# A macaron layer with mixture-of-experts halves: blank stores per attention group, and a dense expert sum on VectorE

## The chip, the cores and the metric

The kernel runs on one core of one Trainium2 chip. The metric is device time in microseconds (us), as the median of several executions. One further execution is taken by the hardware profiler; its page and its trace are the views that this document reads. In them PE is TensorE's products, PEld its weight loads (they lie beside the products), DVE is VectorE, ACT is ScalarE, POOL is GpSimd and SP is SyncE, which here only issues transfers. An engine name with a q (SPq) is that engine's own queue of instructions, from which transfers are started.

## The reference, cut to what matters

The input x holds 8 sequences of 256 tokens of 128 numbers. A feed-forward half with experts, attention, and the same feed-forward half again are added to it:

```python
def ffn(xt):                                   # xt: 2048 tokens x 128
    scores = softmax(xt @ router_w)            # 8 experts
    weights, idx = top_k(scores, 2)            # the two best
    h = gelu(einsum('td,edf->tef', xt, w1)) * einsum('td,edf->tef', xt, v1)   # F = 352
    y = einsum('tef,efd->ted', h, w2)
    return sum(weights[:, :, None] * take_along_axis(y, idx[:, :, None], 1), 1) + bias

x = x + 0.5 * ffn(layernorm(x))
x = x + attention(layernorm(x))                # 16 heads of 8, rotary, alibi, softmax
x = x + 0.5 * ffn(layernorm(x))
```

So each token needs only two of the eight experts, and the kernel may choose between computing those two alone and computing all eight and weighting six of them with zero.

## The kernel before, in words

**Stages.** Two feed-forward parts (part 0 and part 1) stand around attention. The tokens are kept in four blocks of 512 (two sequences each, `xb` and `x2`); a tile is 128 tokens. The expert weights are all in SBUF (`wall`), with F padded to three columns of 128.

**A part by rows.** For a block, `ffn_prep` computes the layer norm (`ln_stats`, with a power on GpSimd; `ln_apply`; `ln_turn`, which transposes on TensorE) and then `route` (L694) picks two experts per token, works out a row number for each choice, and GpSimd scatters the normalised token (`xs<-rows`, an indirect transfer, L731) into the region of its expert in a DRAM buffer `xs`. `wave` (L816) turns the counts into a table of tiles. `Tiles` (L908 to L1034) then runs one tile of 128 rows after another, each of one expert: SP loads it (`xr<-xs`), TensorE transposes it (`xT`), VectorE copies that expert's weights (`ws`, L958), TensorE makes g and v, ScalarE applies the Gelu (`gs`), VectorE multiplies, TensorE makes y (L988), ScalarE scales by the row's weight (`yo`), and GpSimd scatters the row to its token's place in a second DRAM buffer `ys` (L999). Since the number of rows of an expert is known only on the chip, the region's places without a token must hold harmless rows: they point at spare places of `ys`. `no_rows_anywhere` (L647) fills a whole region of part 1's `xs` with such blank rows, 1105 KB in one store from the tile `blank`, one store for each of the 8 experts, issued from SP's queue. The scatters of part 1 (L731) must follow these stores.

**The first sequence.** Part 0 doesn't wait for routing to begin with: sequence 0 (two tiles, unit (0, 0, 2) of `UNITS`) goes through all eight experts in `all_experts` (L745 to L783) while the other sequences are normalised and routed. This makes 16 products, k = 2e + t for expert e and tile t. Each has six products for g and v (`dg`, `dv`), a Gelu on ScalarE and a multiplication on VectorE (`dgs`), and three products into `dy`, in the one bank of tag O of the PSUM pool `ps_c`. `share` holds each token's weight for each expert, zero where the expert was not chosen. Before the change, ScalarE copies `dy` times `share` into `dyo` in SBUF (pool tag yg, two buffers, one for each expert), and when both tiles of an expert are there TensorE adds them to the running sum `dsum` (the bank of tag C) by a product with the identity. One VectorE addition puts `dsum` on the tokens at the end.

**Attention** runs as 32 groups, n = 0 to 31, four heads of one sequence each (`group`, L1202): s on TensorE, a bias and a minimum on VectorE (`ex<-s,alibi`), an exponential on ScalarE, transposes `eT`, copies `et`, then o on TensorE, evacuated by ScalarE (`og`), transposed and normalised by VectorE (`os`). After the fourth group of a sequence, `after` (L1283) makes the output projection `pr` and starts part 1's routing. Before a block can enter attention, its rows of part 0 are gathered: `ffn_sum` (L1036) loads `yg<-ys` on SP's queue and VectorE adds the two expert rows of each token to `xb` (`xb<-xb,yg`); `post1` (L1055) then makes the layer norm and `att_prep` (L1078) makes q, k and v. In the main loop (L1321 to L1345) `post1` of block b is planned with group 8b - 8 (block 1 with group 0), and the second half of block 0 with group 0.

**What sets the order.** Nothing runs as it is written. Each call only notes an operation with an engine, an estimated duration (`us`), an estimated landing time for transfers (`lands`) and a due time; `Plan` (L180 to L313) then schedules them: it takes, on every engine, the operation that can start earliest by its model, and among those that can start about as early, the one with the least due time (`plan.due`, set by `at(...)` or directly, in group numbers for attention). `plan.needs = [scored[n]]` says that what follows is planned after the s products of group n; it binds the planner's model alone and leaves no wait in the program. The engines then run their lists in that order, and the real waits are the data's. `Hand` (L317 to L347) records the operations, so most instructions of the trace have line L334. A buffer or PSUM bank that is taken again gives a wait as well.

The eight blank stores are noted in the main loop when n = 2:

```python
if n == 2:
    for e in range(E):
        no_rows_anywhere(part1, e)
```

Of the kernel before, what the change touches and what calls it, by code (L numbers as in the profile page):

```python
# [8 lines left out]
F32 = mybir.dt.float32  # L9
I32 = mybir.dt.int32  # L10
U32 = mybir.dt.uint32
AF = mybir.ActivationFunctionType
ALU = mybir.AluOpType
AX = mybir.AxisListType

P = 128
D = 128
E = 8
# [47 lines left out]
def tile_macaron(  # L66
# [22 lines left out]
    work = ctx.enter_context(tc.tile_pool(name="work", bufs=2))  # L89
# [3 lines left out]
    ps_c = ctx.enter_context(tc.tile_pool(name="ps_c", bufs=1, space=PS))  # L93
# [86 lines left out]
    class Plan:  # L180
# [33 lines left out]
        def group(self, us):  # L214

            plan = self

            class Group:
                def __enter__(self):
                    plan.one = Op(None, us, plan.due, 0.0)  # L220
                    plan.one.needs.update(plan.needs)
                    plan.ops.append(plan.one)
                    plan.due += plan.pace
                    return plan.one

                def __exit__(self, *_):
                    plan.one = None

            return Group()
# [85 lines left out]
    plan = Plan()  # L315
# [33 lines left out]
    te = Hand(nc.tensor, PE, 0.21)  # L349
    ve = Hand(nc.vector, DVE, 0.22)  # L350
    sc = Hand(nc.scalar, ACT, 0.3)
    gp = Hand(nc.gpsimd, POOL, 0.7)
    sy = Hand(nc.sync, SP, 0.5)
# [10 lines left out]
    def new(pool, shape, dtype, tag, name, bufs=None):  # L364
        def make():
            return pool.tile(shape, dtype, tag=tag, name=name, bufs=bufs)

        if plan is None:
            return make()
        return Late(Root(  # L370
            make, (pool.name, tag), bufs or pool.bufs, pool in (ps_a, ps_b, ps_c)
        ))
# [6 lines left out]
    def together(us):  # L379
        return plan.group(us) if plan is not None else nullcontext()  # L380
# [25 lines left out]
    def at(due, pace=0.0):  # L406

        plan.due, plan.pace = due, pace

    def fixed(shape, name):  # L410
        return new(const, shape, F32, name, name)
# [16 lines left out]
    for e in range(E):  # L428
# [5 lines left out]
        for c, cut in enumerate(CUTS):  # L434
# [4 lines left out]
                us=0.7, lands=8.0 if e < 4 else 12.0,  # L439
# [13 lines left out]
    ident = fixed([P, P], "ident")  # L453
# [30 lines left out]
    for b in range(NBLK):  # L484
        t = fixed([P, 2, TT, RW], f"rows{b}")
# [161 lines left out]
    def no_rows_anywhere(part, e):  # L647

        region = part.xs[REG * e : REG * (e + 1), :].rearrange("(n p) d -> p n d", p=P)
        own = blank[:, SPARE + e, :].unsqueeze(1).to_broadcast([P, REG // P, RW])  # L650
        part.blanked.append(sy.dma_start(region, own, us=0.5, lands=12.0 + 5.0 * e))

    def choose(part, n, xnT, tag):

        pl = scratch(f"rl_{tag}")[:, : n * E].rearrange("p (t e) -> p t e", e=E)
        for t in range(n):
            te.matmul(
                pl[:, t, :], xnT[:, t * P : (t + 1) * P], rw, start=True, stop=True, us=0.47
            )

        full, pair = [P, n, E], [P, 2, n, E]

        def some(name, shape, dtype=F32, bufs=None):
            return new(work, shape, dtype, f"r_{name}", f"r_{name}_{tag}", bufs)

        best, whose = some("best", full), some("whose", full, U32)
        with together(0.1 * n):
            for t in range(n):
                ve.max(best[:, t, :], pl[:, t, :])
        with together(0.14 * n):  # L670
            for t in range(n):
                ve.max_index(whose[:, t, :], best[:, t, :], pl[:, t, :])
        ex = some("sc", full)
        pick = some("pick", pair)
        for k in range(2):
            ve.tensor_tensor(
                pick[:, k], whose[:, :, k : k + 1].to_broadcast(full),
                experts.unsqueeze(1).to_broadcast(full), ALU.is_equal, us=0.15,
            )
        ve.tensor_tensor(ex, best, best[:, :, 0:1].to_broadcast(full), ALU.subtract)  # L680
        part.exps.append(sc.activation(ex, ex, AF.Exp, us=0.25))
        return pick, ex, some

    def halves(n, ex, some, out):

        sm = some("sm", [P, n])
        ve.tensor_reduce(sm, ex, AX.X, ALU.add)
        ve.reciprocal(sm, sm)
        ve.scalar_tensor_tensor(
            out.rearrange("p k t -> p t k"), ex[:, :, 0:2], 0.5,  # L690
            sm.unsqueeze(2).to_broadcast([P, n, 2]), ALU.mult, ALU.mult,
        )
# [52 lines left out]
    def all_experts(part, n, xt, xnT, tag):  # L745

        pick, ex, some = choose(part, n, xnT, tag)
        full, pair = [P, n, E], [P, 2, n, E]
        two = some("two", [P, 2, n])
        halves(n, ex, some, two)  # L750
        prod = some("prod", pair)
        ve.tensor_tensor(prod, pick, two.unsqueeze(3).to_broadcast(pair), ALU.mult)
        share = some("share", full, bufs=1)
        ve.tensor_tensor(share, prod[:, 0], prod[:, 1], ALU.add)
        total = new(ps_c, [P, n, D], F32, "C", "dsum")
        for e in range(E):
            yo = new(work, [P, n, D], F32, "yg", f"dyo{e}", 2)
            for t in range(n):
                k = n * e + t
                at(DUE_DENSE + NEXT_DENSE * k)  # L760
                pg = new(ps_a, [P, 3, P], F32, "A", f"dg{k}")
                pv = new(ps_a, [P, 3, P], F32, "A", f"dv{k}")
                for i, p in enumerate((pg, pv)):
                    with together(0.64):
                        for c in range(3):
                            te.matmul(
                                p[:, c, :],
                                wall[:, e, i * F + CUTS[c] : i * F + CUTS[c] + P],
                                xnT[:, t * P : (t + 1) * P], start=True, stop=True,
                            )  # L770
                gs = new(work, [P, 3, P], F32, "et" if k % 2 else "wide", f"dgs{k}", 8)
                sc.activation(gs, pg, AF.Gelu, us=0.49)
                ve.tensor_tensor(gs, gs, pv, ALU.mult, us=0.56)
                py = new(ps_c, [P, D], F32, "O", f"dy{k}")
                with together(0.66):
                    for c in range(3):
                        te.matmul(
                            py, gs[:, c, :], wall[:, e, 2 * F + c * D : 2 * F + (c + 1) * D],
                            start=(c == 0), stop=(c == 2),
                        )  # L780
                sc.activation(yo[:, t, :], py, AF.Copy, scale=share[:, t, e : e + 1], us=0.37)
            te.matmul(total, ident, yo, start=(e == 0), stop=(e == E - 1), us=0.41)
        ve.tensor_tensor(xt, xt, total, ALU.add, us=0.42)  # L783

    def ffn_prep(part, b, t0, n, xt, eng):

# [345 lines left out]
    for u, (b, t0, t1) in enumerate(UNITS):  # L1132
        at(DUE_UNITS[u], 0.1)
        ffn_prep(part0, b, t0, t1 - t0, xs0[b][:, t0:t1, :], sc)
        n = 2 * b + t1 // 2
# [35 lines left out]
    part1 = Part(1, NB)  # L1171
# [4 lines left out]
    plan = None  # L1176
# [3 lines left out]
    plan = Plan()  # L1180
# [140 lines left out]
    for n, (s, j) in enumerate(steps):  # L1321
        if j == 0:
            o = new(work, [P, 2, D], F32, "o", f"os_{s}", 3)
        last = group(n, s, j, o, ())

        plan.needs = [scored[n]]
        if n == 0:
            plan.due, plan.pace = 0.5, 0.018
            post1(0, ve, slice(1, 2))
            att_prep(1, ve)  # L1330
        if n == 2:
            for e in range(E):
                no_rows_anywhere(part1, e)
        for b in range(1, NBLK):
            if n == max(0, 8 * b - 8):
                plan.due, plan.pace = 8.0 * b - 8, 0.122
                post1(b, gp)
        if j == 0 and 1 < s + 1 < NB:
            plan.due, plan.pace = n + 0.2, 0.043
            att_prep(s + 1, gp)  # L1340
        plan.needs = []
        if j == 3:
            plan.due, plan.pace = n + 2.2, 0.046 if s + 1 == NB else 0.12
            after(s, o)
        plan.pace = 0.0  # L1345
# [9 lines left out]
    plan = None  # L1355
# [63 lines left out]
```

## Time and profile before

| what | value |
|---|---|
| median of 3 runs | 426.54 us (425.74 to 426.95) |
| the profiled execution | 423.09 us |
| its span, first to last instruction | 421.1 us |
| mean granted TensorE clock | 0.971 |
| PE busy | 376.8 us, 89% of the span |
| DVE busy | 314.0 us, 75% |
| ACT busy | 293.2 us, 70% |
| POOL busy | 241.4 us, 57% |
| dense sequence and part 0's tiles, 10 to 132 us | PE busy 117.37, DVE 84.19, ACT 73.04, POOL 66.99 |
| attention, 132 to 325 us | PE busy 179.35, DVE 169.88, ACT 173.72, POOL 122.12 |
| part 1's tiles, 325 to 405 us | PE busy 77.71, DVE 46.93, ACT 42.39, POOL 44.35 |
| end, 405 to 421 us | PE busy 0.56, DVE 5.54 |

The rows by stage are sums over a stretch of the span. How lines of the profile are read: on the page, a row of digits has one digit for each fortieth of the span (10.5 us), the busy share in tenths; PEclk is the TensorE clock that was granted, in tenths of full speed, and DMA the busy share of the 16 transfer engines. A row of the timeline gives the start in us, the length in us, the engine, the line, the operation with out<-in and the shapes, and in brackets how long the engine had been idle and what released it; "x8" gathers eight instructions in succession, whose length then runs from the first to the last. The chain that ended last is spread over many engines here (PE 11% of the span is its largest entry), so no single engine carries the whole kernel, and each stage is read by itself.

### The profile page before, as it was taken

The page shows a single profiled execution, that of the slowest core. Times are in us where ns is not written, and L with a number is a line of the kernel's source. Part 1 is how long each engine was busy: PE and PEld are TensorE (multiplying, and loading weights), DVE is VectorE, ACT ScalarE, POOL GpSimd, SP SyncE. Part 2 cuts the span into 40 slices and gives each one's busy share as a digit, 9 for nine tenths or more (in the row PEclk, how much of TensorE's full clock was granted, in tenths as well). Part 3 has the DMA queues.
Part 4 walks back from the last instruction along what each step waited for, and adds up shares of the span by engine and source line. Part 5 has one row for each costly group of instructions (what it writes and reads, how often), then busy time and mean ns, then how long its engine had stood idle before and what let it go on. Part 6 is the DMA issues. An engine that isn't in the chain of part 4 may idle for free. (4 is left out here: it accounts for less than half of the span.)

```text
span 421.1 us, 11473 instructions
## 1 busy us (share of the span) xinstructions
PE 376.8 (89%) x3456; PEld 317.2 (75%) x3456; DVE 314.0 (75%) x1348; ACT 293.2 (70%) x720; POOL 241.4 (57%) x323
## 2 busy tenths in 40 slices
PE   2989989999997789979999989999998999999940
PEld 1989979999996556755677666766667998999940
DVE  7766658888554898947998989899998677555515
ACT  3887555555555889965999989999999474555520
POOL 5267474547643086345857897687437757435430
PEclk9999989999999999996999999999999999999985
DMA  7971142211211999980000000011101222322117
GB/s 239 279 160 57 51 106 75 71 56 46 79 39 36 241 212 210 212 165 0 2 2 25 30 0 2 2 53 28 28 2 45 71 58 67 85 62 61 37 48 284
DMA packets 45053, 35.05 MB, mean 83 GB/s; under 512 B 4672, under 2 KB 41024, under 8 KB 44992
## 3 DMA queue, kind: packets, MB, share of 16 engines
q1 hardware_dynamic: 38608, 23.61, 25.7%
q0 software_dynamic: 4096, 8.46, 6.1%
q10 hardware_dynamic: 2288, 2.24, 1.5%
q8 instruction: 30, 0.49, 0.5%
q14 instruction: 31, 0.25, 0.2%
HBM read 14.27 MB, written 20.02 MB: 81 GB/s over the span
## 5 line engine op out<-in xcount | busy, mean ns | idle before, releaser
L334 ACT ACTIVATE ex<-ex,least 128x256 f32<-128x256 f32 x256 | 113.4, 508 | 4.8 <-DVE least L334 4.8
L999 POOL DMA_INDIRECT ys<-yo,xr x68 | 67.4, 991 | 63.0 <-ACT yo L334 50.3
L334 DVE CUSTOM_DVE_ANT_0 ex<-s,alibi 128x256 f32<-128x256 f32 x256 | 92.1, 418 | 8.1 <-PE s L334 7.2
L334 PE MATMUL eT<-ident,ex 128*128 128x128 f32 x512 | 74.2, 281 | 5.4 <-ACT ex L334 3.2
L731 POOL DMA_INDIRECT xs<-rows,r_at_f x60 | 58.7, 978 | 35.1 <-issue 14.4
L334 PEld LDWEIGHTS eT<-ident,ex 128*128 128x128 f32 x512 | 57.1, 142 | 24.6 <-ACT ex L334 8.9
L334 DVE TENSOR_TENSOR gs<-gs,v 128x384 f32<-128x384 f32 x68 | 37.3, 549 | 33.7 <-PE xT L334 25.0
L988 PE MATMUL y<-wall,gs 128*128 x408 | 57.2, 276 | 1.8 <-ACT yo L334 1.0
L334 PE MATMUL g<-xTs,ws 128*128 128x128 f32 x408 | 57.6, 278 | 1.0 <-DVE ws L958 1.0
L334 PE MATMUL v<-xTs,ws 128*128 128x128 f32 x408 | 57.3, 277 | 0.0
L334 PEld LDWEIGHTS g<-xTs,ws 128*128 128x128 f32 x408 | 51.7, 194 | 2.1 <-DVE ws L958 0.9
L988 PEld LDWEIGHTS y<-wall,gs 128*128 128x128 f32 x408 | 50.9, 192 | 3.0 <-ACT yo L334 1.4
L958 DVE COPY ws<-wall 128x704 f32 x68 | 37.4, 550 | 19.5 <-DVE gs L334 8.4
L334 PEld LDWEIGHTS v<-xTs,ws 128*128 128x128 f32 x408 | 51.7, 194 | 0.0
L334 ACT ACTIVATE gs<-g 128x384 f32<-128x384 f32 x68 | 33.3, 490 | 21.1 <-PE g L334 21.0
L334 ACT ACTIVATE yo<-y,xr 128x128 f32<-128x128 f32 x68 | 25.0, 368 | 31.3 <-PE y L988 28.4
L359 ACT COPY et<-eT 128x512 f32<-128x512 f32 x79 | 43.7, 583 | 3.7 <-PE eT L334 3.6
L334 PE MATMUL s<-kT,qT 32*128 32x256 f32 x512 | 40.7, 406 | 3.8 <-DVE least L334 3.1
L334 PEld LDWEIGHTS s<-kT,qT 32*128 32x128 f32 x512 | 25.4, 186 | 13.2 <-issue 6.1
L334 PE MATMUL o<-et,vp 128*32 128x256 f32 x512 | 35.1, 393 | 0.0
L334 POOL TENSOR_SCALAR qT<-qa,mask 128x256 f32<-128x256 f32 x32 | 29.8, 944 | 7.4 <-ACT qa L334 7.3
L359 DVE COPY et<-eT 128x512 f32<-128x512 f32 x49 | 32.3, 681 | 1.1 <-PE eT L334 1.0
(167 smaller groups left out, 596.3 us busy)
## 6 DMA issues: line engine op xcount, KB each, us to landing
xs<-blank SPq DMA_DIRECT2D x8, 1105.0 KB, 17.4
xr<-xs SPq DMA_DIRECT2D x68, 65.0 KB, 1.8
yg<-ys SPq DMA_DIRECT2D x3, 512.0 KB
wall<-in_w_dram SPq DMA_DIRECT2D x8, 176.0 KB, 5.1
wall<-in_v_dram SPq DMA_DIRECT2D x8, 176.0 KB, 3.0
yg<-ys SPq DMA_DIRECT2D x5, 256.0 KB
ys<-yo,xr POOLq DMA_INDIRECT x68
yg<-ys ACTq DMA_DIRECT2D x4, 256.0 KB, 4.6
```

The source lines that it names most:

```text
L334: lambda: f(*[real(x) for x in a], **{n: real(x) for n, x in k.items()}),
L359: (nc.scalar.copy if op.eng is ACT else nc.vector.tensor_copy)(real(out), real(in_))
L731: nc.gpsimd.indirect_dma_start(out=part.xs, in_=real(row), in_offset=None, out_offset=bass.IndirectOffsetOnAxis(ap=real(to)[:, k, t : t + ...
L958: nc.vector.tensor_copy(real(ws), flat(w, 2 * F))
L988: nc.tensor.matmul(real(py), real(hT)[:, c, :], flat(w + 2 * F + c * D, D), start=(c == 0), stop=(c == 2),)
L999: nc.gpsimd.indirect_dma_start(out=self.part.ys, in_=real(yo), in_offset=None, out_offset=bass.IndirectOffsetOnAxis(ap=real(xr)[:, D : D + ...
```

## The change

The change has two independent parts.

First, the blank stores of part 1. They were noted all eight at n = 2, in the planner's eyes after the s products of group 2, with landing times from 12 to 47 us. Now one is noted with each of the groups n = 2 to 9, due at n, each with a landing time of 9. Number, size, source and queue of the stores are the same.

Second, the sum over the experts of the first sequence. Before, ScalarE scaled each of 16 `dy` into `dyo`, TensorE added 8 times over the identity into `dsum`, and VectorE added `dsum` to the tokens. Now VectorE multiplies each `dy`, read from its PSUM bank, by the tokens' share and adds the tokens to it in one instruction (`scalar_tensor_tensor`, 16 of them, 128x128 each). `dyo`, `dsum`, the scalings, the identity products and the last addition are gone. The sixteen additions go to the same token tile in turn, expert after expert.

```diff
@@ -648,7 +648,7 @@
 
         region = part.xs[REG * e : REG * (e + 1), :].rearrange("(n p) d -> p n d", p=P)
         own = blank[:, SPARE + e, :].unsqueeze(1).to_broadcast([P, REG // P, RW])
-        part.blanked.append(sy.dma_start(region, own, us=0.5, lands=12.0 + 5.0 * e))
+        part.blanked.append(sy.dma_start(region, own, us=0.5, lands=9.0))
 
     def choose(part, n, xnT, tag):
 
@@ -752,9 +752,7 @@
         ve.tensor_tensor(prod, pick, two.unsqueeze(3).to_broadcast(pair), ALU.mult)
         share = some("share", full, bufs=1)
         ve.tensor_tensor(share, prod[:, 0], prod[:, 1], ALU.add)
-        total = new(ps_c, [P, n, D], F32, "C", "dsum")
         for e in range(E):
-            yo = new(work, [P, n, D], F32, "yg", f"dyo{e}", 2)
             for t in range(n):
                 k = n * e + t
                 at(DUE_DENSE + NEXT_DENSE * k)
@@ -778,9 +776,10 @@
                             py, gs[:, c, :], wall[:, e, 2 * F + c * D : 2 * F + (c + 1) * D],
                             start=(c == 0), stop=(c == 2),
                         )
-                sc.activation(yo[:, t, :], py, AF.Copy, scale=share[:, t, e : e + 1], us=0.37)
-            te.matmul(total, ident, yo, start=(e == 0), stop=(e == E - 1), us=0.41)
-        ve.tensor_tensor(xt, xt, total, ALU.add, us=0.42)
+                ve.scalar_tensor_tensor(
+                    xt[:, t, :], py, share[:, t, e : e + 1], xt[:, t, :], ALU.mult, ALU.add,
+                    us=0.3,
+                )
 
     def ffn_prep(part, b, t0, n, xt, eng):
 
@@ -1328,9 +1327,9 @@
             plan.due, plan.pace = 0.5, 0.018
             post1(0, ve, slice(1, 2))
             att_prep(1, ve)
-        if n == 2:
-            for e in range(E):
-                no_rows_anywhere(part1, e)
+        if 2 <= n < 2 + E:
+            plan.due = n
+            no_rows_anywhere(part1, n - 2)
         for b in range(1, NBLK):
             if n == max(0, 8 * b - 8):
                 plan.due, plan.pace = 8.0 * b - 8, 0.122
```

## The prediction on record

> **What bounds the kernel now.** I read the page's slices first, then busy time in windows, then the waits and the timeline at the two places where TensorE's clock falls. The slices show the dense product of the first sequence and part 0's tiles (10 to 132 us) with PE at 9 nearly throughout, attention (133 to 325) with PE and DVE both near 9, and one hole in slice 18, just where DMA falls from 9 to 0:
>
> ```profile
> PE   2989989999997789979999989999998999999940
> ...
> DVE  7766658888554898947998989899998677555515
> ...
> PEclk9999989999999999996999999999999999999985
> DMA  7971142211211999980000000011101222322117
> ```
>
> The windows (PE, PEld, DVE, ACT, POOL busy us, then clock, DMA share, GB/s) show both falls of the clock. DVE is busy for 1.99 and 2.33 of 5 us while the transfers drain:
>
> ```profile
> 55.00:60.00 5.00, 3.07 (x21) 2.78 (x20) 2.86 (x13) 3.33 (x8) 3.78 (x5) 0.89 0.60 133
> 60.00:65.00 5.00, 5.00 (x35) 4.90 (x35) 2.39 (x5) 1.85 (x6) 2.92 (x4) 0.77 0.33 88
> ...
> 180.00:185.00 5.00, 5.00 (x56) 3.42 (x52) 1.99 (x8) 4.53 (x14) 3.05 (x6) 1.00 1.17 213
> 185.00:190.00 5.00, 2.65 (x20) 1.77 (x16) 2.33 (x9) 2.12 (x6) 1.31 (x3) 1.00 0.28 103
> 190.00:195.00 5.00, 4.22 (x18) 2.60 (x19) 4.97 (x27) 2.18 (x6) 1.42 (x3) 0.70 0.00 0
> 195.00:200.00 5.00, 5.00 (x37) 3.40 (x36) 2.43 (x15) 3.10 (x8) 4.56 (x9) 0.62 0.00 0
> ```
>
> The timeline names the wait: block 2's expert rows (yg), queued on SP behind all eight blank stores.
>
> ```profile
> 136.73 37.02 SPq L334 DMA_DIRECT2D xs<-blank  x8
> 173.89 6.09 SPq L334 DMA_DIRECT2D yg<-ys  x2
> ```
>
> ```profile
> 187.67 0.69 DVE L334 TENSOR_TENSOR xb<-xb,yg 128x512 f32<-128x512 f32 x1 [5.32 <-DMA yg<-ys]
> ```
>
> **Change 1: the blank stores.** The group number is only the planner's: in the built order these stores wait for no engine, only for older transfers on their semaphores. So they aren't paced; SP still issues them back to back. What moves is one transfer: the order becomes yg of block 1, yg of block 0's second half, seven stores, yg of block 2, the eighth store, yg of block 3. VectorE's list in attention is the same row for row. No store is added.
>
> Price of a store: the eight and the loads among them occupy the queue from 136.7 to 187.7, 51 us. The 1.3 MB of yg take about 3.7 us of it at the 350 GB/s of 138 to 140 us; 47.3/8 = 5.9 us a store. Block 2's rows then land 5.9 us sooner relative to the attention, at 181.8 on the old scale. VectorE has its previous work done at 182.35, so the 5.32 us wait should vanish with 0.6 us to spare. Behind it goes what the wait caused: TensorE sat idle for 2.12 us before 189.11, its clock fell, and VectorE waited another 2.57 us for the slow projection (pr) at 199.38. Together 7.9. The check: the evacuations of o (og) of groups 7 to 9 start at 185.46, 198.54 and 203.59, 18.13 us for two groups; the other groups take 5.44 on average (181.49 us from first to last without the gaps of 13.08 and 10.63, over 29), so 18.13 - 10.88 = 7.2 is lost. I take **7.2** (bounds 5.3, the wait alone, and 9: groups 7 to 11 by the two best averages). What is late next: VectorE itself, and GpSimd with block 2's layer norm, which starts as much sooner. The eighth store and block 3's rows land some 3 us later at worst; the first reader of either, a scatter, runs at 222, and block 3's rows are added at 233.
>
> **Change 2: the dense sum.** Removed from TensorE: eight sums over the identity, 16 matmul passes. Their durations (380 ns) overlap, so I take the distance to the next start: 0.54, 0.54, 0.44, 0.43, 0.44, 0.44, 0.54, 0.43, **3.8 us** in all. Removed from ScalarE: 16 scalings at 0.36 = 5.8 us. Added to VectorE: 16 scale-and-adds of 128x128 out of PSUM; this form isn't in the trace. The 128x8 scale-and-add takes 0.16, the 128x256 addition of dsum out of PSUM 0.42, so 0.29 by the line between them (ends 0.16 and 0.42): 4.6 us, less the one 0.42. VectorE is busy 28 of 40 us there (15 to 55), so it can hold them, but in order: each waits for its product, and the next product for it, since their bank has one buffer.
>
> Does TensorE use the 3.8? Two sums (1.08) lie before 36 us, where ScalarE's table loads (1.28 each, at 25.15, 27.94, 32.56, 34.10) set the pace. In the built order the third block's power follows two scatters on GpSimd instead of one (1.26 later), so its normalised rows and the table loads behind them come later, while ScalarE's lost scalings there (0.6) pull the other way. TensorE's product after the third block's transposes, at 35.94 now, I put 0.75 later (between 0.75 later and 1.08 sooner). From there six sums remain, 0.44 + 0.43 + 0.44 + 0.44 + 0.54 + 0.43 = 2.72, and TensorE is the bound: +2.0 so far.
>
> Then the handover to the tiles. Now the sum at 57.99 waits 1.93 us for a scaling behind two table loads:
>
> ```profile
> 57.99 0.70 PE L334 MATMUL dsum<-dyo,ident 128*128 128x256 f32 x2 [1.93 <-ACT dyo L334]
> 58.53 1.15 PE L334 MATMUL dy<-wall,dgs 128*128 128x128 f32 x6
> ```
>
> The clock falls and the products up to 62.25 run slowly: dy 0.95 instead of 0.67 between starts, g and v 1.28 each, the transpose 0.21 instead of 0.13; 1.6 us lost. The loads stay, but the last dense product waits for a Gelu, not a scaling, and one more product and its hidden half stand before it: I estimate a wait of 1.1 (0 to 2.1), so 0.8 back, and the clock's 1.6, since a 1.63 us gap at 141.04 left it at 1.00. Sum: 2.0 + 0.8 + 1.6 = **4.4** (bounds -1 and 6.5). From tile 3 on TensorE runs at 2.12 us a tile until 132, so the gain is carried to attention; tile loads (each 1.8 us, some 1.5 apart from 50.0) stay ahead of it.
>
> **Sum.** 7.2 + 4.4 = 11.6. The profiled execution took 423.09 (span 421.1, 2 us around it), so 411.5 for its like; the median is 426.54, 3.5 higher, and I give it there: **414.9**.
>
> **The clock rule.** The row: the clock fell after gaps of 1.93 and 2.12 us. [...]
>
> **Rivals.**
> - *The rows are still late.* The DMA share falls slowly, 0.93 at 184.5 to 0.06 at 188: the transfer engines end at different times, and the slowest decides. For it speaks that slope and the thin 0.6 us; against it that the slowest also skips a store. If the wait stays by half with its clock fall, 3 to 4 us are lost: 418.5; wholly: 422.1. [...]
> - *The dense stage gains nothing.* ScalarE's loads and VectorE's order absorb the 2.72, or the clock falls at the handover all the same (1.6): 426.5 - 7.2 = 419.3, or 416.5.
> - *Slower: VectorE starves TensorE.* Each expert choice is a burst of about 2.3 us on VectorE (23.20 to 25.5). A product whose bank waits behind a burst leaves TensorE idle; from gaps of about 1.9 us on, the clock falls too, 1.6 more. There are four bursts; if all of them did both, 4 x 3.9 = 15.6 lost against 11.0 gained (7.2 and 3.8): 431.1. Against it: 2 to 4 us of other products stand between most such neighbours in the built order.
> - *Nothing to see:* the yg stays late and the dense gain is lost: 426.
>
> **Chances** (0.3%, 1.3 us, is about what can be told from no change). Forecast 0.56 (own range 411.5 to 418), dense stage gives nothing 0.13, rows still late 0.14, nothing 0.06, slower 0.11. Faster 0.83, same 0.06, slower 0.11. The range: below, all bounds at their best give 426.5 - 15.5 = 411; above, the late rows at 422.
>
> **What would show it.** Right: no DVE wait for yg at group 8 above 1 us; og 7 to og 9 in 11 to 12 us; no clock below 0.9 from 185 to 200; the first s product near 129; scale-and-adds of 0.29. Wrong: VectorE still waiting for yg, a clock fall before 60, TensorE waits above 2 us at third-block transposes, or s later than 132.

## The result and the profile after

| | median | runs |
|---|---|---|
| before | 426.75 us | 425.74 to 428.26, 4 runs |
| changed | 420.71 us | 419.29 to 421.36, 4 runs |

The ratio is 0.9851, 95% interval 0.9811 to 0.9891: the change saves 6.0 us. The forecast was 11.6 saved (414.9). The time lies in the stated range of 411 to 422, but only in the part that the rival of the late rows had added to it: the forecast's own range ended at 418. The gain is half of what was forecast. The profiled execution took 421.11, span 419.3.

Four lines of the page's slices (a digit for 10.5 us):

```profile
PE   2989989999997799989999989999999999999930
...
DVE  7778777889454798958899989899998776555515
...
PEclk9989999999998799996999999999999999999995
DMA  8971143311311999991001000011001222322117
```

The hole in PE's eighteenth digit (178 to 189 us) has gone from 7 to 8 and not closed, and PEclk still has the 6 right behind it. The sixth digit of PEclk, the handover, went from 8 to 9; but there are new falls in the third (an 8, near 28 us) and in the thirteenth and fourteenth (8 and 7, 134 to 144 us). The windows (busy us of PE, PEld, DVE, ACT, POOL, then clock, DMA share, GB/s) give the two stretches that the prediction looked at, and one of the new falls (140 to 145):

```profile
55.00:60.00 5.00, 3.56 (x32) 3.32 (x31) 3.23 (x14) 2.64 (x7) 3.78 (x5) 1.00 0.48 124
60.00:65.00 5.00, 4.93 (x44) 4.69 (x43) 3.79 (x13) 2.60 (x7) 3.78 (x5) 1.00 0.49 114
140.00:145.00 5.00, 4.93 (x42) 2.73 (x42) 4.66 (x28) 4.37 (x11) 0.62 (x1) 0.66 1.24 182
180.00:185.00 5.00, 5.00 (x54) 3.37 (x53) 1.38 (x4) 4.74 (x14) 3.31 (x7) 1.00 1.11 260
185.00:190.00 5.00, 3.46 (x18) 1.90 (x16) 4.63 (x22) 2.26 (x5) 0.18 (x1) 0.83 1.04 193
190.00:195.00 5.00, 5.00 (x29) 3.44 (x32) 4.47 (x26) 2.73 (x7) 3.72 (x5) 0.50 0.04 14
```

The clock fall at the handover (55 to 65 us) is gone: 1.00 against 0.89 and 0.77. From 185 to 195 there is a fall again, 0.83 and 0.50 where the profile before had 1.00 and 0.70, and DVE is busy for 1.38 of the 5 us from 180, less than the 1.99 before. The timelines of SP's queue and of VectorE say why:

```profile
134.59 35.60 SPq L334 DMA_DIRECT2D xs<-blank  x7
170.32 6.18 SPq L334 DMA_DIRECT2D yg<-ys  x1
176.54 0.72 SPq L334 DMA_DIRECT2D xs<-blank  x1
```

```profile
185.37 0.69 DVE L334 TENSOR_TENSOR xb<-xb,yg 128x512 f32<-128x512 f32 x1 [3.96 <-DMA yg<-ys]
```

The order in the queue is the one forecast, seven stores, the rows, one store; and VectorE still waits 3.96 us for the rows. Counted from the issue of the first store, they landed after 50.8 us here (185.37 - 134.59) and after 50.9 in the profile before (187.67 - 136.73): one store fewer ahead, and no sooner.

| step | before | after |
|---|---|---|
| tile 0's transpose xT | 55.79 | 56.50 |
| tile 3's transpose | 64.83 | 61.88 |
| first s product | 133.22 | 130.77 |
| og of group 0 | 143.46 | 142.61 |
| og 7 to og 9 | 18.13 | 16.16 |
| og of group 31 | 324.95 | 322.22 |
| last product y | 404.62 | 402.03 |
| end of span | 421.1 | 419.3 |

By these two profiles the change gains only 1.8 us, while the medians differ by 6.0. So the profiled execution of before was itself 3.5 us better than the median of its kernel, and what is to be found out is where those 3.5 us lie. In the first two sets of runs below the kernel before took 470 to 471 us, with standstills of several engines (last section); only ratios within a set are compared.

### The profile page after: what moved, and what is told of

Read it like the earlier page. It is cut to its first block, busy times and chain, and to the rows that moved or that the text cites. A ratio compares the mean times of both kernels' runs of the same rounds, so it can differ in the third digit from the quotient of the medians.

```text
span 419.3 us, 11415 instructions
## 1 busy us (share of the span) xinstructions
PE 375.8 (90%) x3440; PEld 315.6 (75%) x3440; DVE 318.5 (76%) x1363; ACT 288.3 (69%) x704; POOL 241.5 (58%) x323
## 5 line engine op out<-in xcount | busy, mean ns | idle before, releaser
L334 PE MATMUL eT<-ident,ex 128*128 128x128 f32 x512 | 75.1, 284 | 5.4 <-ACT ex L334 3.1
L334 ACT ACTIVATE gs<-g 128x384 f32<-128x384 f32 x68 | 33.3, 490 | 20.4 <-PE g L334 19.6
L334 PE MATMUL s<-kT,qT 32*128 32x256 f32 x512 | 41.7, 418 | 2.4 <-DVE least L334 1.5
L334 PEld LDWEIGHTS s<-kT,qT 32*128 32x128 f32 x512 | 25.9, 193 | 12.2 <-issue 6.4
```

What stands on the lines that cost most here:

```text
L334: lambda: f(*[real(x) for x in a], **{n: real(x) for n, x in k.items()}),
```

## The experiments

Theory: (1) a blank store costs about 6 us in SP's queue, in a typical execution of before the rows came some 5 us later than in the one that was profiled, and the stores make nearly the whole gain; (2) the dense sum gains 2 to 3 us at the first s, and little at the end. Rivals: the dense sum makes most of the gain; or the rows are late because the stores take the transfer engines, not because of their place in the queue.

**First set (before 471.1 us).** The kernel before, unchanged:

> The kernel before once more, unchanged. Its profiled execution took 423.09, 3.5 us under the median of 426.5. Theory A (the drain of the blank stores varies from one execution to the next, and the execution that was profiled had a short one): this profile takes about 426.5, and the wait for block 2's rows (yg) is longer than the 5.32 us of the first profile, 7 to 9. Theory B (the difference is elsewhere, for instance in where the clock falls): the wait is again 5 to 6 us and the 3.5 us show in other stretches, such as clock falls at other times.

Measured: 0.9983 (0.9952 to 1.0013). VectorE's wait for the rows:

```profile
212.01 0.69 DVE L334 TENSOR_TENSOR xb<-xb,yg 128x512 f32<-128x512 f32 x1 [10.18 <-DMA yg<-ys]
```

The wait is almost twice that of the first profile; og 7 to og 9 took 23.6 us instead of 18.13. The rows landed 56.3 us after the first store's issue (212.01 - 155.68), not 50.9. This speaks for theory A; but the execution also had standstills, which the first profile had not and neither theory names, so a third profile was taken below.

The stores alone (the dense part as before the change):

```diff
-        part.blanked.append(sy.dma_start(region, own, us=0.5, lands=12.0 + 5.0 * e))
+        part.blanked.append(sy.dma_start(region, own, us=0.5, lands=9.0))
...
-        if n == 2:
-            for e in range(E):
-                no_rows_anywhere(part1, e)
+        if 2 <= n < 2 + E:
+            plan.due = n
+            no_rows_anywhere(part1, n - 2)
```

> The stores of the change alone; the dense sum stays on ScalarE and TensorE. Theory A (one store fewer ahead of the rows is worth its share of the queue, and a typical execution of before waits longer than the profiled one): 3.5 to 4.5 us faster than before, so about 422.5, with a wait for yg of 2 to 5 us left. Theory B (the stores are worth only the 2.0 us that group 7 to group 9 gained between the two profiles): 424.5. My prediction had 7.2: 419.3 and no wait.

Measured: 0.978 (0.9708 to 0.9852). The wait fell from 10.18 to 1.64 us, og 7 to og 9 from 23.6 to 12.0, the rows landed after 50.1 us. The stores alone give as much as the whole change gave (0.9851 above, 0.9841 in the next set). A wait is left, as theory A has it, though under its 2 to 5 us; the gain, 7.4 us between the medians, is above both theories and near the 7.2 of the prediction.

The dense sum alone (the second part of the change, all eight stores at n = 2):

> The dense sum of the change alone; all eight stores stay ahead of block 2's rows. Theory A: the first s product comes 2.5 us sooner (130.8), and the time gains that or less, 424.0 to 425.0, because the eight stores start with the attention and the wait for yg moves with it. Theory B (the dense sum makes most of the measured 6.0 us): 421.5 to 422.5. My prediction had 4.4: 422.1.

Measured: 0.9993 (0.9958 to 1.0029), wait for the rows 10.31 us. The first s came at 154.24, later than before's 152.19. Theory B is out; that the standstills hid a gain can't be told from this run.

The rows ahead of all stores, with both parts of the change:

```diff
+        if n == 1:
+            plan.due = 1.0
+            for b in 2, 3:
+                ahead[b] = ffn_sum(part0, b)
+                next(ahead[b])
...
-            for _ in ffn_sum(part0, b, q):
+            for _ in ahead.pop(b, None) or ffn_sum(part0, b, q):
```

> Both parts of the change, and block 2's and block 3's rows loaded ahead of all eight stores (noted at group 1). If it is the place in SP's queue behind the stores that makes block 2's rows late, VectorE's wait for yg (3.96 us in the profile after) is gone, the distance from og 7 to og 9 falls from 11.3 and 4.9 us (16.2) to 11 or 12, no clock fall is left from 185 to 195, and the time is 4 to 5 us below after: 416. If the wait only uncovers another (GpSimd's layer norm of block 2, the shared transfer engines), the wait for yg goes and the sum of og 7 to og 9 stays above 14: 419 to 420.7. If the stores, now started some 10 us later, make part 1's scatters late, the time is 421 or more.

Measured: 0.9757 (0.9704 to 0.981). The two additions of the rows ran at 201.47 without a wait, og 7 to og 9 took 10.8 us, and no clock fall is left in that stretch (170 to 290 us all at 1.00). With no store ahead of them the rows are in time, and nothing else is late there. The stores started 10 us later (166.28 against 156.48 in the changed kernel's run of the next set) and nothing waited for them.

**Second set (before 470.2 us).** Before once more, and the changed kernel:

> The kernel before again, to see a third execution. In the first profile VectorE waited 5.32 us for block 2's rows, in the second 10.18, and there ScalarE also stood still four times for 3 to 7 us with nothing in the trace that released it. Theory A (the stores' drain varies): without such standstills the time is about 426 and the wait for yg lies between 5 and 10 us. Theory B (the drain is long only where ScalarE stands still): without standstills the wait is 5 to 6 us, with them about 10.

> The changed kernel again, on the same chip as the others of this call. Theory A: 6 to 9 us under before (the stores' 7.4 of the run with the stores alone, and the dense sum's 0 to 2.5); og 7 to og 9 at 12 to 16 us. If the dense sum adds to the stores in full, og 0 comes 2 us sooner than in before; if it gives nothing, og 0 comes as in before and the difference is that from og 7 to og 9 alone.

Measured: 0.9981 (0.9948 to 1.0013) and 0.9841 (0.979 to 0.9892). The wait in before was 10.19 us, the rows landed after 56.1 us; in the changed kernel 1.51 and 48.7. og 7 to og 9: 22.3 and 12.2. The first s came at 153.85 and 152.76, og 0 at 165.36 and 164.70. So here too the gain is the stretch of the rows. Both executions of before with the long wait had standstills, so these two alone don't exclude theory B (a long drain only with standstills); the drain of the stores in the executions without standstills, given below with the price of a store, does.

The dense sum alone, again:

> The dense sum alone, again. In the first run of it ScalarE stood still for 9.3, 5.0 and 6.2 us before 81 us, 20.4 in all against 17.6 in before, and the first s came at 154.2 against 152.2; the time was 0.9993 of before. Theory A (the product chain gains 2.5 us and the standstills hid it): without standstills the first s comes 2 to 3 us sooner than in before and the time is 1.5 to 2.5 us less. Theory B (VectorE's order takes back what TensorE saves): within 1 us of before, whether there are standstills or not.

Measured: 1.0017 (0.9972 to 1.0062), first s at 154.60, wait for the rows 8.16. There were standstills again (ScalarE 9.3, 5.0 and 4.0 us before 82 us), so its two theories weren't told apart.

Rows first, and two PSUM banks for dy:

```diff
-                py = new(ps_c, [P, D], F32, "O", f"dy{k}")
+                py = new(ps_c, [P, D], F32, "C" if k % 2 else "O", f"dy{k}")
```

> Rows of blocks 2 and 3 ahead of all stores, as before in this study, and the dense products dy in two PSUM banks by turns (the bank of the sum that is gone is free), so that a product needn't wait for VectorE's scale-and-add of the one before. If one bank is what holds the dense stage back, tile 0's transpose and the first s come another 1 to 1.5 us sooner than in the changed kernel (its wait of 1.44 us for VectorE at 58.21 goes) and the time is 3 to 5 us under the changed kernel; if the products wait for their own halves (dgs) all the same, the first s stays within 0.5 us and only the rows' gain of 3 us is left.

Measured: 0.976 (0.9691 to 0.983), first s at 150.34, the earliest of all with standstills. But ScalarE stood still for 8.8 us before 77 us here and for about 18 to 21 in the runs with one bank, so this first s says little about the bank.

**Third set (before 429.3 us, no standstill in any of its four profiles).**

The rows first (the edit above, and one store per group), with the dense sum of before:

> The rows of blocks 2 and 3 ahead of all eight stores, and the dense sum left on ScalarE and TensorE. Against the same order of loads with the dense sum on VectorE (0.9757 of before) it prices the dense part where no store is in the way. Theory A (the dense sum on VectorE is worth nothing with one PSUM bank for dy, since each product waits for VectorE's scale-and-add): 0.973 to 0.979 of before, the first s within 1.5 us of before's. Theory B (it is worth the 2.5 us at the first s of the profile after): 0.980 to 0.984.

Measured: 417.40 us, 0.9735 (0.9701 to 0.9769). The four stores ahead, with both parts (the load noted at n == 6 instead of 1):

> Both parts of the change with four stores ahead of the rows of blocks 2 and 3, and four behind. In the profiles so far block 2's rows landed 56.1 to 57.2 us after the first store was issued with eight stores ahead (50.9 in the very first profile), and 48.7 to 50.8 with seven. If a store costs 6 us in the queue, they land at 30 to 34 us, 15 us before VectorE asks for them, so the wait is gone and the time equals that with none ahead, 0.976. If the rows are late for another reason (the transfer engines shared with the stores), a wait of 1 us or more stays and the time is that of the changed kernel, 0.984.

Measured: 416.50 us, 0.9714 (0.9676 to 0.9752). SP's queue and VectorE in this kernel:

```profile
134.96 16.88 SPq L334 DMA_DIRECT2D xs<-blank  x4
151.95 7.20 SPq L334 DMA_DIRECT2D yg<-ys  x2
159.20 22.58 SPq L334 DMA_DIRECT2D xs<-blank  x4
```

```profile
178.98 1.87 DVE L334 TENSOR_TENSOR xb<-xb,yg 128x512 f32<-128x512 f32 x2
```

No bracket: VectorE didn't wait, though four more stores were still being written. The last packet of the rows of blocks 2 and 3 ended at 168.25, 33.3 us after the first store's issue, where 30 to 34 were expected. The windows of this kernel show no fall of the clock, with DMA shares above 1:

```profile
180.00:185.00 5.00, 4.74 (x51) 3.09 (x50) 4.93 (x23) 5.00 (x15) 4.02 (x7) 1.00 1.31 174
185.00:190.00 5.00, 4.58 (x54) 3.43 (x53) 4.96 (x27) 4.40 (x12) 3.85 (x8) 1.00 1.18 191
190.00:195.00 5.00, 5.00 (x58) 3.39 (x54) 4.87 (x26) 4.95 (x14) 4.94 (x7) 1.00 0.24 47
```

So stores that are being written behind the rows don't make them late; what makes them late is the number of stores ahead of them. That is as far as the rival of the shared transfer engines is tested: whether the same rows, loaded through another engine's queue beside the stores, would be in time was not tried. And the two kernels of this pair, neither with a late row, give a price for the dense sum, though they differ in the order of the transfers too: first s at 133.18 without it and 130.90 with it, 2.3 us sooner; og 0 at 143.57 and 142.16, 1.4; last y at 397.86 and 396.77, 1.1; the medians 0.9 apart, with intervals that overlap. Theory A for the first of them (worth nothing) had the ratio right; theory B (2.5 us of time) had the first s right and the time wrong. What the time has is about 1 us or nothing. The kernel with the rows first and two banks, below, has the same order of transfers as the first of them, and the new dense sum; between these two the first s comes 2.3 us sooner (133.18 and 130.92) and the medians lie 1.3 apart (417.40 and 416.09), again with intervals that overlap.

The two banks, with the stores as changed, and with the rows first:

> The changed kernel with the dense products dy in two PSUM banks by turns, and the stores as changed (seven ahead of block 2's rows). If the one bank holds the dense stage, the first s comes 2 to 3 us sooner than in the changed kernel and the time is about 0.977 of before (0.984 less 2 to 3 us); if the sooner first s of the run with two banks and the rows first (150.3 against 152.8 to 154.6) was chance, it is 0.982 to 0.986.

> Rows first and two banks, again. Its two numbers did not agree: a median of 457.1 (3 rounds), 13 us below before's, and a ratio of 0.976. If the two banks add to the rows' gain: 0.969 to 0.974 of before, first s at 150 to 151. If they add nothing: 0.976 to 0.980 and first s at 153 or later.

Measured: 423.55 us, 0.9864 (0.9827 to 0.99), first s at 130.09; and 416.09 us, 0.9686 (0.9659 to 0.9713), first s at 130.92. Against 130.77 (profile after) and 130.90 (four ahead) with one bank the second bank gives 0 to 0.8 us at the first s: one bank isn't what holds the dense stage. (The first s of 150 expected for the second kernel was meant for executions with standstills. Its ratio falls on the side of "they add", but its interval overlaps that of four ahead with one bank, 0.9676 to 0.9752.) The first of the two is also a second case of seven stores ahead without standstills:

```profile
186.05 0.69 DVE L334 TENSOR_TENSOR xb<-xb,yg 128x512 f32<-128x512 f32 x1 [6.17 <-DMA yg<-ys]
```

The rows landed after 52.0 us (186.05 - 134.09). It and four ahead differ in the place of the rows (and in the bank, worth little): 0.9864 against 0.9714, 6.4 us of 429.3. That is what the change leaves on the table.

The rows first with two banks, 416.09 us, beats both kernels: 13 us under before, where the change has 6. Neither part of the change was run alone without standstills; that the stores make nearly the whole gain rests on the two sets with them and on the stretch from og 7 to og 9.

## Why the prediction was half right

*The order of the transfers* was right: the stores aren't paced, and one transfer moved past one store.

*The price of a store*, 5.9 us, came out near, in part by luck. Landing of the rows (the start of the addition that waited for them) after the first store's issue, over all profiles in which VectorE waited for them:

| stores ahead | us after the first store's issue |
|---|---|
| 8 | 50.9 (the profile shown first), 56.3, 56.1, 57.2, 56.1 |
| 7 | 50.8 (the profile after), 50.1, 48.7, 52.0 |

The means are 50.4 with seven and, without the first profile, 56.4 with eight: 6.0 a store. But the last four with eight all had standstills, and of those with seven only the second and third, so the packets of the stores themselves are the better measure (17,408 of 520 bytes, 2,176 a store). From the end of the first store's packets to the end of the sixth's, a store took 5.4 us in the profile before, 6.2 in the profile after, and 6.0 to 6.6 in the eleven other profiles in which no rows lie between these six. The windows of the profiles before and after show it in GB/s, the last number:

```profile
145.00:170.00 25.00, 22.85 (x225) 15.39 (x224) 23.64 (x115) 22.75 (x60) 18.15 (x28) 1.00 1.23 211
145.00:170.00 25.00, 23.31 (x230) 15.94 (x229) 23.64 (x112) 23.08 (x60) 18.48 (x29) 1.00 1.25 184
```

At these rates 1105 KB take 5.4 and 6.1 us. The prediction's 5.9 was counted from the first issue to VectorE's addition, over a drain that was a fast one (the packets of its eight stores ran for 45.3 us, 5.7 a store): too long a stretch at too fast a rate, which offset each other. Without standstills a store took 6.2 to 6.6 us (four profiles), with them 6.0 to 6.3: the long drain doesn't need them. Why the drain of the first profile was fast is not known.

*The step that failed* is the one behind it: "Block 2's rows then land 5.9 us sooner relative to the attention, at 181.8 on the old scale", so that the wait "should vanish with 0.6 us to spare". The old scale was that of one execution, and in it the rows came 5.5 us sooner than in four others. That the profiled execution lay 3.5 us under the median was seen, and carried along as a constant. It was no constant: eight stores at 5.4 instead of 6.1 us each (the mean of the four others with eight ahead) make 5.6 us, about the 5.5, and they lie in the very wait that the change moves. With eight stores ahead og 7 to og 9 took 18.13 us in that profile and 20.3 to 23.6 in the other four, 22.2 on average, 4.1 more. All four had standstills. A second execution of before without them was not profiled; that its drain is long too is an inference, from the 6.2 to 6.6 us a store of the other kernels' profiles without standstills, and from the third set: there the rows in time gained 0.0265 of 429.3, 11.4 us, without the dense sum, where the first profile had only 18.13 - 10.75 = 7.4 to give. The difference of 4.0 is about the 3.5 between that execution and its median. From a typical execution the sum would have run: 56.4 - 5.9 = 50.5 after the first store, against VectorE being ready for the rows after 45.6 (182.35 - 136.73 in the first profile); so a wait of about 5 stays. That is the rival "the rows are still late", which had 0.14 and, by half and wholly, 418.5 and 422.1 us; the measured 420.71 lies between these. In all four profiles with seven stores ahead the wait stayed, 1.5 to 6.2 us; 3.96 in the profile after, with a fall of the clock behind it.

What lateness costs in all was near the estimate's shape: og 7 to og 9 without any wait takes 10.5 to 10.8 us in the five profiles with the rows in time (10.88 was expected). In the four executions with eight stores ahead and standstills 22.2 - 10.8 = 11.4 us are lost, as much as the rows alone gain in the third set. Change 1 takes about half of it (to 16.2 in the profile after; 12.0 to 19.3 in the three others with seven stores ahead), and that is about the whole 6.0.

*The dense sum*: 4.4 was forecast for attention's start, 2.45 came in the profile after (130.77 against 133.22), and 2.3 between the two kernels of the third set. Term by term: the product after the third block's transposes came at 36.89, 0.95 later (0.75 expected). The clock fall at 27.87, which the prediction didn't have, cost nothing there: with four ahead, which has the same dense stage and no fall, the product came at 36.99, after a wait of 0.99 for ScalarE. The six sums behind it went, but one product waited 1.03 us at 48.54 where 0.46 was lost before:

```profile
47.43 0.59 DVE L957 COPY ws<-wall 128x704 f32 x1 [0.48 <-issue]
47.95 0.54 DVE L334 TENSOR_TENSOR dgs<-dgs,dv 128x384 f32<-128x384 f32 x1
48.54 0.94 PE L334 MATMUL dy<-wall,dgs 128*128 128x128 f32 x6 [1.03 <-DVE dgs L334]
```

Its half (dgs) stood in VectorE's list behind the copy of a tile's weights (ws), before which VectorE itself was idle for 0.48 us; the expert choice came behind it, at 48.41. So it was the order in VectorE's list and not a full VectorE, though each scale-and-add took 0.35 us instead of 0.29. At the handover the wait is 1.44 (1.1 expected; the product's bank came free with a scale-and-add, behind a half that had waited 1.28 for its Gelu) and the clock stayed at 1.00, as expected (no fall there in the four profiles without standstills that have the new dense sum; one at 58.88 and 58.92 in the two that have the old one):

```profile
56.50 0.27 PE L334 MATMUL xT<-ident,xr 128*128 128x128 f32 x1
58.21 0.94 PE L334 MATMUL dy<-wall,dgs 128*128 128x128 f32 x6 [1.44 <-DVE x L334]
58.99 0.27 PE L334 MATMUL xT<-ident,xr 128*128 128x128 f32 x1
```

At tile 3 the gain was 2.95, at tile 4 2.6. "The gain is carried to attention" held to the first s and not behind it: in the profile after, the clock fell at 133.68 and again at 140.51, and og 0 was 0.85 sooner; in the third set, without these falls, og 0 was 1.4 sooner, because block 1's rows, loaded once part 0's last rows are written, were issued 1.9 sooner (134.01 against 135.94) and landed 1.4 sooner (138.10 against 139.51). At the end about 1 us is left. The rival "VectorE starves TensorE" showed in this one place, through a weight copy and not an expert choice, without a fall of the clock there, and was not what decided.

*The clock*: a fall at the handover was priced at 1.6 and went away; the three new falls of the profile after were not in the forecast. Up to 400 us the clock stood at 0.50 in these stretches: in the profile before from 58.88 for 3.41 us and from 192.00 for 6.83; in the profile after from 27.87, 133.68 and 140.51 for 3.41 us each, and from 188.29 for 6.83. The two starts of before lie 133.12 us apart, and the later three of after lie 105.81, 112.64 and 160.42 us behind its first; in lengths of the shortest fall, 3.41 us, these are 39.0, and 31.0, 33.0 and 47.0. The prediction's "from gaps of about 1.9 us on, the clock falls too" rested on two gaps and doesn't hold: the longest waits of TensorE in the 3.41 us ahead of the four falls of after were 0.54, 0.84, 1.60 and 0.94 us, while 1.44 us at 58.21, and 1.63 at 141.04 in the profile before, brought none. Nor does the busy time tell it: TensorE was busy for 1.5 to 2.6 us of the 3.41 ahead of each of the six falls, and with 1.82 us busy from 185.17 to 188.59 in the profile before no fall began at 188.59. What brings a fall was not shown.

## What to carry to other kernels

Where a profiled execution lies apart from the median of its kernel, find the stretch in which it differs before adding or subtracting in it; here the load behind eight stores landed after 50.9 us in one execution and after 56 to 57 in four others, and it was this wait that the change moved. A load that a late stage needs belongs ahead of the bulk stores in its queue, not one store further up: count the stores that fit between the queue's start and the moment of need (here four ahead left no wait, seven left 1.5 to 6.2 us). Work taken from the engine that bounds a stage and given to one that serves it in order is worth only what the receiving engine's order leaves, here 2.3 of 3.8 us at the next stage, and about 1 us or nothing at the end.

## What the runs showed that was not expected

In the first two sets the same kernel took 470 to 471 us, and 427 to 429 otherwise. The record names chip 4 for the first set, chip 13 for the second, and chip 4 again for the third, so the chip alone doesn't explain it. In every profile of the first two sets, and in none of the others, ScalarE and VectorE stood still at nearly the same moment, with a releaser that the profile can't name, as in the first set's before:

```profile
39.55 0.37 ACT L334 ACTIVATE dyo<-dy,r_share_f 128x128 f32<-128x128 f32 x1 [4.24 <-remote]
```

```profile
39.47 0.19 DVE L334 TENSOR_TENSOR r_row_f<-rp_f,r_next_f 128x32 f32<-128x32 f32 x1 [5.54 <-remote]
```

The products that both read had been made 5 us before (from 32.56 and 32.93 on). In the three runs of the old dense sum the standstills sit largely at the same instructions; with the new one at others near them. GpSimd went on with its scatters meanwhile until 38 us. Their cause was not found, and no experiment was made on it.

The scale-and-add out of PSUM (128x128) took 0.349 us on average over 16, more than the line between a 128x8 and a 128x256 form gave (0.29).
